# Two float32r pieces instead of three bf16 ones in the last pair's products

## The chip, the cores and the metric

The kernel runs on one core of a Trainium2 chip. The core's engines work side by side, each through its own queue in order: TensorE (PE in the profile; PEld is its weight load), VectorE (DVE), ScalarE (ACT), GpSimd (POOL), and SyncE (SP), which issues most DMAs. The metric is the device time of one execution in microseconds; of several runs the median is given. One further execution was profiled, and all rows of a profile are of that one.

## The reference

Four graph layers run over x, 8 batches of 2048 nodes with 64 features, with one adjacency matrix of 2048 x 2048 for all batches. The first three are attention layers. The last one, which the change is about, is cut to this:

```python
def _L3_gnn_ref(x, w0, b0, wa, ba, adj):
    feat = jax.nn.softplus(x * (INV_SQRT2 * w0[0, 0]) + b0[0])
    scores = feat * wa + ba
    mask = adj > 0
    logits = scores[:, None, :, :] * mask[None, :, :, None].astype(scores.dtype)
    logits = jnp.where(mask[None, :, :, None], logits, jnp.float32(-1000000000.0))
    attn = jax.nn.softmax(logits, axis=2)
    return jnp.einsum('bijd,bjd->bid', attn, feat)

x = _layernorm(x + _L3_gnn_ref(x, ...), axis=-1)
```

The score of a neighbour j depends on j and the feature alone. So softmax and sum become two products of the 0/1 mask: numerator = mask x (feat * exp(score)), denominator = mask x exp(score), for each feature, and the output is their quotient (plus a term for nodes without neighbours), followed by the residual and the layer norm.

## The kernel before, in words

P is 128, N 2048, K = N / P = 16, K2 = 8, F = 64. The mask lies in SBUF as `edge`, fp8, [128, 16, 2048]: block row jb, all target nodes. It is transposed, so that a block `edge[:, jb, ib*128:(ib+1)*128]` can stand in TensorE as the weights for target nodes ib.

The last layer goes by pairs of batches (0,1), (2,3), (4,5), (6,7). `l3_features(b)` (line 1070) computes softplus, exp and their product for one batch into a float32 tile `vf` of [128, 16, 2, 64] (numerator and denominator side by side), and then splits it into three bf16 pieces `v0`, `v1`, `v2`: ScalarE casts to bf16, VectorE or GpSimd subtracts the piece, ScalarE casts the rest, and the second rest is the third piece. GpSimd subtracts for the even batch of a pair, VectorE for the odd one (line 1119). The two batches fill the halves of the same tiles. With a 0/1 mask, three bf16 pieces give nearly the full float32 sum. The pieces of the first three pairs lie in tiles of their own; those of pair (6,7) lie in the `w` buffers (four, of 8 KB per partition), which the attention layers leave free at the end: three of them are taken. The generator waits for that point by `now[0] < 3` (lines 1102 to 1107).

`l3_products` (line 1131) takes a pair when both batches are ready. For each of the 16 blocks ib of target nodes it adds up 16 x 3 products, 128x128 mask block by 256 columns, in one PSUM tile, and ScalarE evicts it to `nd`. After each two blocks `l3_finish` (line 1177) is added to the background work: GpSimd makes `e` (four small operations), VectorE takes the reciprocal, multiplies and adds, ScalarE squares, VectorE reduces, GpSimd takes the power for the inverse deviation, VectorE scales, SyncE sends two DMAs out. During the last pair PSUM tiles come from a pool of two (`alone`).

Order is written out by hand: every stage is a generator, `Streams.step` (line 1219) lets each living one emit its next piece, and `yield n` passes n turns. Each engine's queue holds the instructions in the order of emission, by the helper at line 78, which is why nearly all rows of the profile say L78. A tile with one buffer (such as tag `e`, used by `softplus` and by `l3_finish`) makes the next writer wait for the last reader. The buffers with tag `row` (two, of 8 KB) hold a row broadcast to all partitions in the attention layers (`prepare`, line 725) and are free in the last pair.

Of the kernel before, what the change touches and what calls it, by code (L numbers as in the profile page):

```python
# [7 lines left out]

F32 = mybir.dt.float32
BF16 = mybir.dt.bfloat16  # L10
U8 = mybir.dt.uint8
FP8 = mybir.dt.float8e4
# [2 lines left out]
ALU = mybir.AluOpType  # L15
AX = mybir.AxisListType

P = 128
# [30 lines left out]
def gnn4_kernel(ctx: ExitStack, tc: tile.TileContext, t, out):  # L49
    nc = tc.nc  # L50
    x_in, adjT = t["x"], t["adjT"]
    B, N, F = x_in.shape
    K = N // P
    K2 = K // 2
# [50 lines left out]
    class Banks:  # L105
# [4 lines left out]
        pool = None  # L110
# [26 lines left out]
    vf_slots, nd_slots, o_slots, lo_slots = (Slots(2) for _ in range(4))  # L137

    pe, dve, act, pool = (InOrder(e) for e in (nc.tensor, nc.vector, nc.scalar, nc.gpsimd))

    def psum(name):
        return pm.tile([P, 512], F32, tag="pm", name=name)

# [3 lines left out]
    def bc_k(v, n=K, f=F):  # L147
        return v[:, None, :].to_broadcast([P, n, f])


    ident = consts.tile([P, P], F32, name="ident")
    make_identity(nc, ident)
    ones = consts.tile([P, P], F32, name="ones")
    nc.gpsimd.memset(ones, 1.0)
    mhalf = consts.tile([P, K], F32, name="mhalf")
    nc.gpsimd.memset(mhalf, -0.5)
# [27 lines left out]
    def rows_tile(pool, tag, name, unit=True):  # L184
        return Rows(pool.tile([P, K * F1 + 1], F32, tag=tag, name=name), unit)

# [9 lines left out]
    work = ctx.enter_context(tc.tile_pool(name="work", bufs=2))  # L196
# [3 lines left out]
    def dram_row(name, eng=nc.sync):  # L200
        v = consts.tile([P, F], F32, name=name + "_bc")
        src = t[name]
        eng.dma_start(v, bass.AP(tensor=src.tensor, offset=src.offset, ap=[[0, P], [1, F]]))
        return v
# [9 lines left out]
    src = t["L0_gnn_a"]  # L214
# [6 lines left out]
    p = psum("p_nodes")  # L221
# [26 lines left out]
    edge = consts.tile([P, K, N], FP8, name="edge")  # L248
    te = consts.tile([P, K, NB], BF16, name="te")
    ones3 = consts.tile([3, P], BF16, name="ones3")  # L250
    nc.gpsimd.memset(ones3, 1.0)
    ones_h = consts.tile([P, 2], BF16, name="ones_h")
    nc.gpsimd.memset(ones_h, 1.0)
    zeros_h = consts.tile([P, 2 * K], BF16, name="zeros_h")
    nc.gpsimd.memset(zeros_h, 0.0)
    emptyT = consts.tile([P, 512], BF16, name="emptyT")
    empty = consts.tile([P, K], F32, name="empty")
# [101 lines left out]
    def softplus(f, y, src):  # L359

        act.activation(y, src, AF.Abs, scale=l3c[:, 0:1], bias=l3c[:, 1:2])
        act.activation(y, y, AF.Exp, scale=-1.0)
        yield 1
        act.activation(y, y, AF.Ln, bias=1.0)
        act.activation(f, src, AF.Relu, scale=l3c[:, 0:1], bias=l3c[:, 1:2])
        yield 1
        dve.tensor_tensor(f, f, y, ALU.add)
# [182 lines left out]
    def mean_pieces(sc, total, n):  # L550
# [3 lines left out]
        pm_slots.give()  # L554
        a = sc.mean = small.tile([P, F], BF16, tag="mean3", name=f"mean3_{n}", bufs=B + 1)
        for i in range(2):
# [503 lines left out]
    def l3_mean(q, i, fs, n):  # L1060

        yield from pm_slots.take()
        p = psum(f"p_fm_{n}")
        pe.matmul(p[:, :F], lhsT=ones, rhs=fs, start=True, stop=True)
        yield 1
        q.fm[i] = small.tile([P, F], F32, tag="fm", name=f"fm_{n}", bufs=4)
        dve.tensor_scalar(q.fm[i], p[:, :F], 1.0 / N, -1.0, ALU.mult, ALU.add)
        pm_slots.give()

    def l3_features(b):  # L1070

        if b % 2 == 0:
            q = Pair()
            q.bs, q.n, q.fm, q.ready = [b, b + 1], f"{b}", {}, 0
            pairs.append(q)
        else:
            q = pairs[-1]
        i = b % 2
        n = f"3_{b}"
        yield from vf_slots.take()  # L1080
        yield from e_slots.take()
        yield from h_slots.take()
        f = tmp.tile([P, K, F], F32, tag="h", name=f"f_{n}")
        y = tmp.tile([P, K, F], F32, tag="e", name=f"sp_{n}")
        yield from softplus(f, y, x_cur[b].v)
        e_slots.give()
        v = late.tile([P, K, 2, F], F32, tag="vf", name=f"vf_{n}", bufs=2)
        pool.tensor_tensor(v[:, :, 1], f, bc_k(wa), ALU.mult)
        pool.tensor_tensor(v[:, :, 1], v[:, :, 1], bc_k(l3off), ALU.add)
        fs = small.tile([P, F], F32, tag="fs", name=f"fs_{n}")  # L1090
        dve.tensor_reduce(fs, f.rearrange("p k f -> p f k"), AX.X, ALU.add)
        bg.add(l3_mean(q, i, fs, n))
        yield 2
        act.activation(v[:, :, 1], v[:, :, 1], AF.Exp)
        yield 1
        dve.tensor_tensor(v[:, :, 0], f, v[:, :, 1], ALU.mult)
        h_slots.give()
        yield 1

        if i == 0:  # L1100
            if b == B - 2:
                while now[0] < 3:
                    yield 1
                q.v = [
                    work.tile([P, K, 2, 2, F], BF16, tag="w", name=f"v{m}_{q.n}", bufs=4)
                    for m in range(3)
                ]
            else:
                yield from v_slots.take()
                q.v = [  # L1110
                    late.tile([P, K, 2, 2, F], BF16, tag=f"v{m}", name=f"v{m}_{q.n}")
                    for m in range(3)
                ]
        else:
            while not hasattr(q, "v"):
                yield 1
        act.copy(q.v[0][:, :, i], v)
        yield 1
        eng = dve if i else pool
        eng.tensor_tensor(v, v, q.v[0][:, :, i], ALU.subtract)  # L1120
        yield 1
        act.copy(q.v[1][:, :, i], v)
        yield 1
        eng.tensor_tensor(q.v[2][:, :, i], v, q.v[1][:, :, i], ALU.subtract)
        vf_slots.give()
        yield 1
        q.ready += 1

    K4 = K // 8

    def l3_products():

        while len(pairs) == 0 or pairs[0].ready < 2:
            yield 1
        yield from Banks.share()
        for m in range(B // 2):
            while pairs[m].ready < 2:
                yield 1
            q = pairs[m]
            for ib in range(K):  # L1140
                if ib % K4 == 0:
                    yield from nd_slots.take()
                    q.nd = late.tile(
                        [P, K4, 2, 2, F], F32, tag="nd", name=f"nd_{q.n}_{ib}", bufs=2
                    )
                alone = now[0] == 3
                if alone:
                    p = Banks.pool.tile([P, 1024], F32, tag="b", name=f"p_l3_{q.n}_{ib}")
                else:
                    yield from pl_slots.take()  # L1150
                    p = psum(f"p_l3_{q.n}_{ib}")
                p = p[:, : 4 * F]
                for jb in range(K):
                    for v in q.v:
                        pe.matmul(
                            p,
                            lhsT=edge[:, jb, ib * P : (ib + 1) * P],
                            rhs=v[:, jb].rearrange("p b i f -> p (b i f)"),
                            start=(jb == 0 and v is q.v[0]),
                            stop=(jb == K - 1 and v is q.v[2]),  # L1160
                        )
                    if jb % K2 == K2 - 1:
                        yield 1
                act.activation(
                    q.nd[:, ib % K4],
                    p.rearrange("p (b i f) -> p b i f", b=2, i=2),
                    AF.Identity,
                    bias=empty[:, ib : ib + 1],
                )
                if not alone:  # L1170
                    pl_slots.give()
                if ib % K4 == K4 - 1:
                    bg.add(l3_finish(q, ib // K4, q.nd))
            if m < B // 2 - 1:
                v_slots.give()
# [110 lines left out]
    for n, (layer, b) in enumerate(todo):  # L1286
        if (layer, b) == (2, 1):
            early_.close()
            late = ctx.enter_context(tc.tile_pool(name="late", bufs=1))
            bg.add(l3_products())  # L1290
# [573 lines left out]
```

## Time and profile before

| | us |
|---|---|
| median of 3 runs | 1573.19 (1572.83 to 1574.51) |
| span of the profiled execution | 1572.4 |
| median above that span | 0.8 |
| TensorE busy | 1322.6 (84%) |
| VectorE busy | 1298.6 (83%) |
| ScalarE busy | 801.3 (51%) |
| GpSimd busy | 812.6 (52%) |
| products of the last layer, 3072 records | 353.9 |

Only instructions are profiled, so the profiled execution's own time is its span and the little that lies around it. Times within the profile count from the start of the span. The busy time of TensorE counts overlapping records; the pace of a run of products is read from when they start, or from when ScalarE evicts their result. "Idle before <-releaser" in a row says what an engine waited for.

### The profile page before, as it was taken

The numbers are of one execution on the slowest core, as the hardware profiler recorded it, in microseconds if no ns is written. First come the engines' busy times: TensorE is split into PE (matmuls) and PEld (weight loads), VectorE is DVE, ScalarE is ACT, GpSimd is POOL, SyncE is SP. The second block draws the span as 40 slices with busy tenths as digits, with TensorE's granted clock in tenths as the row PEclk, the third lists the DMA queues.
The fourth block names the chain that finished last, engine by engine and source line by source line (L and its number), as shares of the span: only waits on it lengthen the run. The fifth ranks groups of instructions, "written<-read, shape, count | busy, mean of one in ns | idle before, by whom it ended". The sixth has DMA issues, their size and how long they took to land.

```text
span 1572.4 us, 20954 instructions
## 1 busy us (share of the span) xinstructions
PE 1322.6 (84%) x8130; PEld 657.3 (42%) x8130; DVE 1298.6 (83%) x1364; ACT 801.3 (51%) x1635; POOL 812.6 (52%) x742
## 2 busy tenths in 40 slices
PE   3568989988899899998878575899977989789996
PEld 3213323333333334333222131455543646477885
DVE  4798989988999999999877878978887888777444
ACT  5225445555575434343488667675766575552110
POOL 1144353334234434232576577687879687864332
PEclk8889999999999999999999688899988999889998
DMA  8710000000000000000000000000100000000000
GB/s 325 222 25 1 1 2 1 1 2 2 1 1 2 0 1 2 2 29 27 0 1 27 27 2 27 1 29 7 35 7 34 1 8 8 8 8 15 14 13 18
DMA packets 42190, 36.86 MB, mean 23 GB/s; under 512 B 37509, under 2 KB 37813, under 8 KB 39906
## 3 DMA queue, kind: packets, MB, share of 16 engines
q1 hardware_dynamic: 41538, 34.26, 7.0%
q8 instruction: 66, 1.08, 0.3%
q10 hardware_dynamic: 544, 1.17, 0.2%
q14 instruction: 42, 0.34, 0.1%
HBM read 30.94 MB, written 4.45 MB: 23 GB/s over the span
## 4 chain that ended last, share of the span: by engine, by line
PE 24%; DVE 21%; ACT 9%; issue 4%; POOL 4%; POOLq 0%; DVEq 0%; ACTq 0%
PE p_l L78 16%; DVE w L78 12%; PE acc L78 7%; ACT e L78 4%; DVE o L78 2%; DVE st_x L78 2%; ACT sp L78 1%; POOL w L78 1%; DVE vf L78 1%; ACT x L78 1%; POOL vf L78 1%; ACT v L78 1%; DVE fs L78 1%; POOL e L78 1%; PE p_o L78 1%
## 5 line engine op out<-in xcount | busy, mean ns | idle before, releaser
L78 DVE SCALAR_TENSOR_TENSOR w<-r,se,edge 128x2048 f32<-128x2048 f32 (+1 forms) x270 | 555.6, 2104 | 22.6 <-PE r L78 19.6
L78 PE MATMUL acc<-w,pv 128*64 128x512 f32 x2048 | 502.9, 623 | 74.9 <-DVE w L78 68.2
L78 PEld LDWEIGHTS <-edge 128*128 128x128 fp8e4 x3842 | 322.3, 99 | 124.8 <-issue 66.4
L78 ACT ACTIVATE e<-w,s_g 128x1024 f32<-128x1024 f32 x256 | 277.8, 1113 | 173.2 <-DVE w L78 128.8
L78 PE MATMUL acc<-w,x 128*64 128x512 f32 x1024 | 284.6, 673 | 89.4 <-DVE w L78 84.3
L78 PE MATMUL p_l<-v,edge 128*128 128x256 bf16 x3072 | 353.9, 276 | 0.6 <-ACT nd L78 0.6
L78 DVE TENSOR_TENSOR w<-e,edge 128x1024 f32<-128x1024 f32 x256 | 299.9, 1213 | 50.4 <-ACT e L78 48.7
L78 POOL TENSOR_SCALAR w<-row,hi_g,lo_g 128x2048 f32<-128x2048 f32 x128 | 275.6, 2159 | 42.6 <-PE acc L78 39.6
L78 PEld LDWEIGHTS acc<-w,pv 128*64 128x64 f32 x2048 | 132.0, 140 | 340.7 <-issue 182.5
L78 PEld LDWEIGHTS acc<-w,x 128*64 128x64 f32 x1024 | 64.4, 146 | 239.2 <-DVE w L78 170.7
L78 ACT ACTIVATE nd<-p_l,empty 128x256 f32<-128x256 f32 x64 | 29.9, 469 | 132.9 <-PE p_l L78 132.9
L78 ACT ACTIVATE x<-o,st_x 128x64 f32<-128x64 f32 x256 | 90.3, 444 | 4.2 <-DVE st_x L78 4.2
L78 ACT COPY oT<-acc 128x512 f32<-128x512 f32 x48 | 25.7, 587 | 126.8 <-PE acc L78 126.8
L78 ACT ACTIVATE o<-p_o,den 128x64 f32<-128x64 f32 x256 | 56.0, 326 | 49.9 <-DVE den L78 49.7
L78 POOL TENSOR_TENSOR st_h<-isw_h,mhalf 128x16 f32<-128x16 f32 x8 | 23.9, 2982 | 106.6 <-DVE isw_h L78 81.7
L78 PE MATMUL p_o<-rh,oT 128*128 128x130 f32 x384 | 60.5, 295 | 20.4 <-DVE st L78 13.2
L78 POOL TENSOR_TENSOR st_x<-isw_x,mhalf 128x16 f32<-128x16 f32 x24 | 71.1, 2964 | 2.0
L78 PEld LDWEIGHTS p_o<-rh,oT 128*128 128x128 f32 x384 | 49.8, 197 | 52.1 <-issue 32.9
L78 DVE TENSOR_REDUCE st<-sq 128x4 f32<-128x256 f32 x32 | 13.2, 414 | 65.2 <-ACT sq L78 65.1
L78 POOL TENSOR_SCALAR isw_x<-isw_x 128x16 f32<-128x16 f32 x24 | 6.3, 263 | 113.5 <-DVE isw_x L78 113.5
L78 POOL CAST rT<-rT 16x128 bf16<-16x128 f32 x45 | 15.1, 335 | 94.6 <-ACT rT L78 91.5
L78 POOL TENSOR_SCALAR isw<-isw 128x4 f32<-128x4 f32 x32 | 7.4, 231 | 104.1 <-DVE isw L78 99.5
(236 smaller groups left out, 1516.5 us busy)
## 6 DMA issues: line engine op xcount, KB each, us to landing
raw<-in_adjT_dram SPq DMA_DIRECT2D x8, 1024.0 KB
raw<-in_adjT_dram SPq DMA_DIRECT2D x16, 512.0 KB
row<-rows_d_g SPq DMA_DIRECT2D x8, 1024.0 KB
x<-in_x_dram SPq DMA_DIRECT2D x8, 512.0 KB
out_dram<-o SPq DMA_DIRECT2D x64, 64.0 KB
row<-row_d ACTq DMA_DIRECT2D x1, 1024.0 KB
row_d<-rT SPq DMA_DIRECT2D x15, 12.0 KB
row<-row_d SPq DMA_DIRECT2D x15, 12.0 KB
```

Source lines behind the costliest of these rows:

```text
L78: ins = f(*args, **kwargs)
```

## The change

For the last pair alone, `l3_features` now makes two pieces, each split in two tiles of half the blocks (four tiles of 8 KB, so all four `w` buffers), of type float32r, a 4-byte type with fewer mantissa bits: ScalarE casts both halves once, VectorE subtracts both halves, for both batches. The products need both operands in that type, so the mask block of each ib (128 x 2048 elements) is cast from fp8 to float32r by a new function `widen`, even ib on ScalarE, odd ib on GpSimd, into the two `row` buffers, one block ahead of its use. The products of this pair are 16 x 2 per ib instead of 16 x 3. In the program a float32r product is a single instruction that brings its weights itself, where the bf16 product has a weight load of its own ahead of it. The other pairs are unchanged; their loop moves into `products`.

```diff
+F32R = mybir.dt.float32r
...
                 q.v = [
-                    work.tile([P, K, 2, 2, F], BF16, tag="w", name=f"v{m}_{q.n}", bufs=4)
-                    for m in range(3)
+                    [
+                        work.tile([P, K2, 2, 2, F], F32R, tag="w", name=f"v{m}_{h}_{q.n}", bufs=4)
+                        for h in range(2)
+                    ]
+                    for m in range(2)
                 ]
...
+        if b >= B - 2:
+            for h in range(2):
+                act.copy(q.v[0][h][:, :, i], v[:, h * K2 : (h + 1) * K2])
+            yield 1
+            for h in range(2):
+                dve.tensor_tensor(
+                    q.v[1][h][:, :, i],
+                    v[:, h * K2 : (h + 1) * K2],
+                    q.v[0][h][:, :, i].bitcast(F32),
+                    ALU.subtract,
+                )
+            vf_slots.give()
+            yield 1
+            q.ready += 1
+            return
...
+    wide = {}
+
+    def widen(ib):
+
+        if ib < K:
+            m = work.tile([P, K, P], F32R, tag="row", name=f"mask_{ib}")
+            src = edge[:, :, ib * P : (ib + 1) * P]
+            if ib % 2:
+                pool.tensor_copy(m, src)
+            else:
+                act.copy(m, src)
+            wide[ib] = m
+
+    def products(p, q, ib, jb):
+
+        if q.bs[1] == B - 1:
+            for m in range(2):
+                pe.matmul(
+                    p,
+                    lhsT=wide[ib][:, jb],
+                    rhs=q.v[m][jb // K2][:, jb % K2].rearrange("p b i f -> p (b i f)"),
+                    start=(jb == 0 and m == 0),
+                    stop=(jb == K - 1 and m == 1),
+                )
+            return
+        for v in q.v:
+            pe.matmul(
+                p,
+                lhsT=edge[:, jb, ib * P : (ib + 1) * P],
+                rhs=v[:, jb].rearrange("p b i f -> p (b i f)"),
+                start=(jb == 0 and v is q.v[0]),
+                stop=(jb == K - 1 and v is q.v[2]),
+            )
...
             q = pairs[m]
+            if m == B // 2 - 1:
+                widen(0)
             for ib in range(K):
+                if m == B // 2 - 1:
+                    widen(ib + 1)
...
                 for jb in range(K):
-                    for v in q.v:
-                        pe.matmul(
-                            p,
-                            lhsT=edge[:, jb, ib * P : (ib + 1) * P],
-                            rhs=v[:, jb].rearrange("p b i f -> p (b i f)"),
-                            start=(jb == 0 and v is q.v[0]),
-                            stop=(jb == K - 1 and v is q.v[2]),
-                        )
+                    products(p, q, ib, jb)
                     if jb % K2 == K2 - 1:
                         yield 1
```

## The prediction

> **What bounds the kernel now.** I read the chain of waits in order of time first, because only its last stretch can belong to the pair of batches that the change touches. The long pieces of its end:
>
> ```profile
> 1403.58 4.03 POOL vf L78
> 1407.63 1.90 ACT v L78
> 1417.22 1.92 DVE fs L78
> 1419.87 138.93 PE p_l L78 x1248
> ```
>
> From 1419.87 us TensorE alone carries the end: 1248 products in a row, with nothing between them. Before that the chain goes through GpSimd (a subtraction of the value pieces of batch 6), ScalarE and VectorE, and the change touches that too. Next, busy time by stretch (PE, PEld, DVE, ACT, POOL with counts, clock, DMA):
>
> ```profile
> 1425.21:1474.80 49.59, 49.59 (x456) 44.46 (x455) 29.26 (x55) 9.50 (x16) 17.00 (x30) 1.00 0.07 15
> 1474.80:1558.60 83.80, 83.80 (x770) 75.03 (x767) 38.10 (x80) 10.03 (x24) 26.28 (x48) 1.00 0.06 14
> 1558.60:1572.40 13.80, 0.18 (x2) 0.00 (x0) 6.33 (x16) 1.20 (x3) 4.55 (x8) 0.61 0.11 24
> ```
>
> The second row is the last pair: TensorE is full at full clock, and ScalarE (12%) and GpSimd (31%) have room. The third is the drain after the last product. ScalarE's evictions in the timeline give the pace:
>
> ```profile
> 1474.98 0.47 ACT L78 ACTIVATE nd<-p_l,empty 128x256 f32<-128x256 f32 x1 [4.77 <-PE p_l L78]
> 1480.22 0.47 ACT L78 ACTIVATE nd<-p_l,empty 128x256 f32<-128x256 f32 x1 [4.46 <-PE p_l L78]
> ```
>
> One row block each 5.24 us; divided by its 48 products that is 109.2 ns, whatever the 273 ns of one record say (they overlap). The pair costs 16 x 5.24 = 83.84 us.
>
> No float32r product is in this trace. Its nearest kin are float32 products, in TensorE's timeline and its weight loads' (a run of instructions each, with its length):
>
> ```profile
> 563.24 0.97 PEld L78 LDWEIGHTS p_s<-as,xTv 128*128 128x128 f32 x8 [0.81 <-issue]
> 563.24 1.06 PE L78 MATMUL p_s<-as,xTv 128*128 128x4 f32 x8
> 608.63 1.94 PE L78 MATMUL acc<-w,pv 128*64 128x512 f32 x8 [0.67 <-ACT oT L78]
> ```
>
> The p_s products stream only 4 columns, so their weight loads set the pace: (0.97 - 0.19) / 7 = 0.111 us per load of 128 float32 columns, 0.19 being one load. The products p_o with 130 columns run at the same 0.11 us (8 in 1.16 us), so a load does hide behind the stream before it. The acc run is 4 products of 512 columns, each in two records, two at a time side by side: (1.94 - 0.59) / 3 = 0.45 us per record, 0.88 ns a column. The bf16 stream takes 109 / 256 = 0.43 ns a column; call that one cycle, and float32 takes two, twice.
>
> **What the Trainium skill says.** FP8 and Floating Point Precision, TensorE Precision Notes: full float32 takes four passes, the reduced form reads 4-byte values and truncates them. The acc run (two records, each two cycles a column) agrees on the four; that the reduced form is one pass of one cycle a column is my reading, shown by no row. TensorE: Matmul & The Clock Gate, Weight-path perf modes: the fast weight load is off for float32. The trace agrees: a 128-column load lasts 190 ns in p_s and 98 ns for the fp8 mask. Same page, What's actually happening: after an idle window of some 3.4 us the clock halves. Here idle stretches of 2.2 to 2.5 us were already mostly followed by 3.4 us at half clock, and the one of 3.83 us at 1415.35 by 6.83 us.
>
> **The change part by part.**
>
> *1. Products.* 48 become 32 per row block, 768 become 512. Each streams 256 columns, the same 109 ns if one cycle a column, with a weight load of 111.7 ns (bound from above by p_s) behind it: I take 111.7. 512 x 0.1117 = 57.2 us instead of 83.84: **-26.65**. From both sides: 109 ns if the loads are faster (another -1.4); 216 ns if 4-byte values stream at two cycles a column, as p_xT's transposes do (8 of 128 columns in 1.09 us).
>
> *2. Mask casts, eight by ScalarE, eight by GpSimd, two buffers.* ScalarE: its cast of 128x2048 (v<-vf) lasts 1.90 us; the page ScalarE: Activation LUTs (What ACT_TABLE_LOAD costs) gives 186 + 0.833 x 2048 ns = 1.89 for the same. Cast ib+1 waits for the last product of ib-1, which is when block ib starts. ScalarE first evicts (0.47): done some 2.6 us into a block of 3.57. Hidden, with 0.9 us to spare; behind a cast that still waits stands only the next eviction, which needs a later product anyway. GpSimd shows no such cast; its one-input pass of the same size:
>
> ```profile
> L78 POOL TENSOR_SCALAR w<-row,hi_g,lo_g x128: 2040/2047/3245, 767.9 to 1351.2; 128x2048 f32<-128x2048 f32 x128
> ```
>
> I take 2.1 us. The floor: GPSIMD Engine Reference, section 3.1, has bodies with few operations at 1.03 cycles an element, at its 1.2 GHz an estimated 1.8 us. The ceiling is the two-input pass here, 4.07 us. GpSimd's queue for two blocks (7.15 us) then holds 2.1 + 0.23 + 1.04 (the power) + 4 x 0.52 (e) = 5.5 us. Behind a waiting cast stand isw and the power of the former rows, and behind those VectorE's scaling and the output; they have 1.4 us to spare. The cover is gone at a cast of about 3.2 us; at 4.07 two blocks take 4.07 + 0.3 + 3.57 = 7.95, +0.8 us seven times. Taken: **0** (ceiling +5.6).
>
> *3. The hand-over to the last pair.* Cast 0 is queued on ScalarE behind the eviction of the former pair's last block (its order in the program, not a need of data). So TensorE stops at 1474.78, the eviction starts at 1474.98, the cast about 0.37 later and ends at 1477.25, the first product starts near 1477.4: **+2.6**. Cast 1 has no such wait. A gap of 2.6 us should bring one 3.4 us window at half clock: **+1.7** (0 to 3.4).
>
> *4. Value pieces.* For batch 6 GpSimd loses two subtractions (4.06 and 4.07 us); VectorE gets two halves (1024 elements, 1.21 each). ScalarE casts two halves once instead of a whole tile twice, and its second cast no longer waits at 1407.63 for GpSimd:
>
> ```profile
> 1407.75 1.58 PE L78 MATMUL p_l<-v,edge 128*128 128x256 bf16 x13
> 1409.95 5.40 PE L78 MATMUL p_l<-v,edge 128*128 128x256 bf16 x48 [0.62 <-ACT nd L78]
> 1419.18 0.69 PE L78 MATMUL p_fm<-fs,ones 128*128 128x64 f32 x2 [3.83 <-DVE fs L78]
> ```
>
> In TensorE's timeline the stop of 0.62 is the eviction behind that cast, the stop of 3.83 the mean of batch 7, which waits for the softplus queued on ScalarE. Its first step (1409.80) then waits only for buffer e, freed by VectorE: 1402.78 + 2 x 1.2 (the new halves) + 1.74 + 0.43 + 0.43 = 1407.8 (the 3.40 us of o<-nd at 1404.48 was contention with GpSimd's subtraction). All that follows moves 2.0 us ahead: the mean at 1417.2, **-2.0** (0 to -4). TensorE then stands 2.8 us instead of 0.62 + 3.83, so one half-clock window instead of two: **-1.6** (0 to -3.3). Batch 7's single round of pieces, and the fourth w buffer, end long before 1474.78, where they are needed (v<-vf at 1433.3 was the last): 0; without that cover some 2 us.
>
> *5. Drain.* Same instructions after the last eviction, 13.6 us: 0. No DMA is added.
>
> Sum: -26.65 + 0 + 2.6 + 1.7 - 2.0 - 1.6 = -25.95 against the profiled 1572.4: 1546.4 us. The median of the runs is 0.8 above the span: **1547.2**, given as 1547.
>
> **The rivals.**
>
> *A. The stream takes two cycles a column.* For it: p_xT, the only one-record float32 stream here, does. Against it: a transpose has to deliver the whole float32 value, and acc's four passes leave a quarter for one. 512 x 0.216 = 110.6 us, +26.8 instead of -26.65: 1600.7 us. Its place is the last pair's stretch, and it decides from 162 ns per product on ((83.84 - 2.6 - 1.7 + 2.0 + 1.6) / 512). Chance 0.15.
>
> *B. GpSimd's cast becomes the bound.* For it: every second block waits on it, in a queue with the power and four adds. Against: 2.05 us for the pass of the same size. Ceiling +5.6: 1553 us; with a cast slower still than two-input work, up to 1560. Chance 0.10.
>
> *C. Weight loads don't hide* (the instruction loads its own weights, so there is no separate load to pull ahead). Against: p_o hides them. 109 + 55 to 109 + 111 ns: 84 to 113 us, 1574 to 1603. Chance 0.04.
>
> *D. The change doesn't do what it says*: float32r runs as full float32, 4 x 109 ns: 223 us, about 1713. The program lists one product, not two, for each. Chance 0.02.
>
> **How the numbers follow.** My forecast has 0.69; its own range is 1541 (cheap loads, no half-clock windows) to 1553. With B the range 1541 to 1566 holds about 0.8. Within 0.2% (about 3 us, what a measurement tells from no change) lies only the low end of C: 0.02. Faster 0.79 (forecast and B), slower 0.19 (A, D, most of C).
>
> **What would show it.** Row blocks in the evictions 3.6 us apart (right), 6.9 (A) or alternating 3.6 and 4.4 (B, with TensorE idle until GpSimd's mask). LDWEIGHTS of the mask near 190 ns at a pitch of 112. One stop of TensorE of 2.6 us before the first product of the last pair, ended by ScalarE's mask. p_fm of batch 7 near 1417. The forecast is wrong if the pitch isn't within 109 to 120 ns or if TensorE stops anywhere inside the last pair.

## The result and the profile after

The changed kernel takes 1552.48 us (median of 4 runs, 1550.31 to 1554.46) against 1573.01 for the kernel before in the same runs; the ratio is 0.9865, with a 95% interval of 0.9828 to 0.9902. It is faster, by 20.5 us, where 26 had been forecast.

The chain of waits of the changed kernel in order of time, its end (start, length, what):

```profile
1401.17 2.81 DVE v L79 x2
1414.10 1.91 DVE fs L79
1416.49 54.08 PE p_l L79 x480
1470.97 1.90 ACT mask L79
1472.91 61.71 PE p_l L79 x512
```

GpSimd's subtraction has left the chain, VectorE's two halves have come in, and the run of products is now cut once, by ScalarE's cast of mask block 0. Busy time by stretch of the changed kernel (PE, PEld, DVE, ACT, POOL with counts, clock, DMA), the same three stretches as before:

```profile
1419.90:1470.40 50.50, 50.50 (x464) 45.14 (x462) 30.82 (x58) 8.04 (x17) 19.91 (x34) 1.00 0.08 17
1472.90:1534.60 61.70, 61.69 (x512) 61.49 (x512) 42.69 (x80) 22.06 (x30) 39.69 (x55) 1.00 0.08 18
1534.60:1548.50 13.90, 0.00 (x1) 0.00 (x0) 6.33 (x16) 1.20 (x3) 4.55 (x8) 0.67 0.10 24
```

The pair now takes 61.7 us instead of 83.8, and its weight loads (second figure) fill the stretch too. The rest of the core is far from full: ScalarE 22 of 61.7 us, GpSimd 39.7. The timeline of ScalarE's evictions gives the pace:

```profile
1477.05 0.48 ACT L79 ACTIVATE nd<-p_l,empty 128x256 f32<-128x256 f32 x1 [3.87 <-PE p_l L79]
1480.88 0.48 ACT L79 ACTIVATE nd<-p_l,empty 128x256 f32<-128x256 f32 x1 [1.58 <-PE p_l L79]
1484.72 0.47 ACT L79 ACTIVATE nd<-p_l,empty 128x256 f32<-128x256 f32 x1 [3.06 <-PE p_l L79]
```

A row block takes 3.84 us; divided by 32 that is 120 ns a product, not the 111.7 of the forecast. The instructions on the mask tiles:

```profile
L79 PEld LDWEIGHTS p_l<-v,mask x512: 186/192/192, 1472.9 to 1534.2; 128*128 128x128 f32 x171
L79 PE MATMUL p_l<-v,mask x512: 279/283/384, 1472.9 to 1534.3; 128*128 128x256 f32 x171
L79 POOL CAST mask<-edge x8: 1885/1892/1892, 1465.2 to 1527.0; 128x2048 fp32r<-128x2048 fp8e4 x8
L79 ACT CAST mask<-edge x8: 1887/1892/1897, 1471.0 to 1523.5; 128x2048 fp32r<-128x2048 fp8e4 x8
```

One record per product, and 120 ns from one to the next: here float32r is a single pass. Both engines cast a block in 1.89 us. TensorE's timeline at the two places where it stops:

```profile
1416.06 0.43 PE L79 MATMUL p_fm<-fs,ones 128*128 128x64 f32 x2 [3.19 <-DVE fs L79]
...
1472.91 57.26 PE L79 MATMUL p_l<-v,mask 128*128 128x256 f32 x475 [2.35 <-ACT mask L79]
```

By stages of the two profiled executions (marks: the last product of the attention layers' sums `acc` ends; p_fm, the mean of batch 7's features, starts; the pair's first product starts; its last one starts; the end):

| stage | before | after | difference |
|---|---|---|---|
| to the last attention product | 1364.46 | 1362.94 | -1.5 |
| to p_fm of batch 7 | 54.72 | 53.12 | -1.6 |
| to the pair's first product | 55.60 | 56.85 | +1.25 |
| the pair | 83.73 | 61.41 | -22.3 |
| drain | 13.89 | 14.18 | +0.3 |
| span | 1572.4 | 1548.5 | -23.9 |

The first row lies ahead of everything that the change moves. In later executions of variants that are equal up to there it ended anywhere from 1361.4 to 1367.0, so it is spread between executions. The third row is the stop at the hand-over (+2.35) against a shorter stretch at half clock around p_fm (3.4 us instead of 6.8), which gives back some 1.1 us.

### The profile page after: what moved, and what is told of

It is laid out like the page before. It is cut to its first block, busy times and chain, and to the rows that moved or that the text cites. A ratio compares the mean times of both kernels' runs of the same rounds, so it can differ in the third digit from the quotient of the medians.

```text
span 1548.5 us, 20475 instructions
## 1 busy us (share of the span) xinstructions
PE 1303.4 (84%) x7874; PEld 645.7 (42%) x7874; DVE 1300.8 (84%) x1366; ACT 812.4 (52%) x1643; POOL 820.2 (53%) x748
## 4 chain that ended last, share of the span: by engine, by line
PE 23%; DVE 22%; ACT 9%; issue 4%; POOL 3%; POOLq 0%; DVEq 0%; ACTq 0%
PE p_l L79 15%; DVE w L79 12%; PE acc L79 7%; ACT e L79 4%; DVE o L79 2%; DVE st_x L79 2%; ACT sp L79 1%; DVE vf L79 1%; ACT x L79 1%; PE p_o L79 1%; POOL w L79 1%; DVE nd L79 1%; ACT v L79 1%; DVE fs L79 1%; POOL vf L79 1%
## 5 line engine op out<-in xcount | busy, mean ns | idle before, releaser
L79 PEld LDWEIGHTS <-edge 128*128 128x128 fp8e4 x3074 | 246.1, 99 | 116.1 <-issue 65.9
L79 PE MATMUL p_l<-v,edge 128*128 128x256 bf16 x2304 | 267.9, 276 | 0.0
L79 PE MATMUL p_l<-v,mask 128*128 128x256 f32 x512 | 61.7, 283 | 2.4 <-ACT mask L79 2.4
L79 PEld LDWEIGHTS p_l<-v,mask 128*128 128x128 f32 x512 | 61.5, 192 | 2.6 <-ACT mask L79 2.6
```

The costliest lines, as they stand in the source:

```text
L79: ins = f(*args, **kwargs)
```

## The experiments

The theory: the gain is the 256 products that are gone; the pieces give a little, the hand-over takes a little, and float32r itself only costs. Its rivals: the gain comes from ScalarE no longer waiting for GpSimd, or from float32r. Beside it stood the question of the 120 ns.

### The changed kernel again

> The changed kernel itself once more, as the level for its neighbours here. Both theories: 1550 to 1554 us, ratio to before 0.985 to 0.988. In the profile the 512 float32r products at a pitch of 120 ns, TensorE standing about 2.4 us before the first of them.

1553.4 us, ratio 0.9869 (0.9847 to 0.9891), pitch (from the start of one product to the next) 120 ns, stop 2.35 us. In its profile p_fm comes 53.12 us after the last attention product and the pair takes 61.41 us, both as in the first. The level holds; the experiments are compared with this and with the first result.

### Two bf16 pieces, no float32r

```diff
-                    for m in range(3)
+                    for m in range(2)
...
+        if b >= B - 2:
+            dve.tensor_tensor(q.v[1][:, :, i], v, q.v[0][:, :, i], ALU.subtract)
+            vf_slots.give()
+            yield 1
+            q.ready += 1
+            return
...
-                            stop=(jb == K - 1 and v is q.v[2]),
+                            stop=(jb == K - 1 and v is q.v[-1]),
```

> The last pair in two bf16 pieces, made as in the change (ScalarE casts once, VectorE subtracts), no third piece: less precise, no float32r, no mask casts. Theory P (the gain is the 256 products that are gone, float32r only costs): 512 products at 109 ns, 55.9 us for the pair instead of 61.4, no stop before it, so some 7 to 8 us below the changed kernel, near 1544. Theory Q (float32r itself or the casts bring the gain): not below the changed kernel.

1542.98 us, ratio 0.982 (0.9797 to 0.9843). Busy time of this run in the stretch of the pair:

```profile
1470.40:1526.40 56.00, 56.00 (x514) 50.04 (x512) 38.07 (x80) 10.01 (x24) 26.26 (x48) 1.00 0.09 20
```

512 products in 56 us (109 ns each), and TensorE does not stop before them. It is 10 us below the changed kernel by the medians; by the stages of the profile 5.6 in the pair and 2.5 ahead of it. So the gain is the number of products (theory P): float32r with its casts costs some 8 us of what two pieces save. What it is meant to buy is precision, since a bf16 piece has fewer bits; no run here measured how much.

### The pieces alone

```diff
-        eng = dve if i else pool
+        eng = dve if i or b >= B - 2 else pool
```

> The kernel before with one part of the change: in the last pair VectorE makes both subtractions of batch 6 too, GpSimd none; still three bf16 pieces. Theory P: the small part of the gain, the mean of batch 7 some 1.5 us earlier and at most one half-clock window less: 1 to 4 us below before. Theory R (most of the gain comes from ScalarE no longer waiting for GpSimd): 10 us or more below before.

1570.9 us, ratio 0.9985 (0.9974 to 0.9995). TensorE's timeline of this run:

```profile
1408.80 5.73 PE L78 MATMUL p_l<-v,edge 128*128 128x256 bf16 x51
1417.38 0.43 PE L78 MATMUL p_fm<-fs,ones 128*128 128x64 f32 x2 [2.85 <-DVE fs L78]
```

The short stop of 0.62 us is gone, the other is 2.85 us instead of 3.83, and p_fm comes 52.8 us after the last attention product instead of 54.7. Theory P's 1 to 4 us; theory R's 10 us are excluded by the interval (0.8 to 4.1 us).

### Cast 0 one block earlier

```diff
-            if m == B // 2 - 1:
-                widen(0)
             for ib in range(K):
+                if m == B // 2 - 2 and ib == K - 1:
+                    widen(0)
```

> The changed kernel with mask cast 0 queued on ScalarE one row block earlier, ahead of the eviction of the former pair's last block. Theory H (the stop of 2.4 us at the hand-over is that queue order alone): the stop is gone, the pair starts 2.4 us earlier, 1.5 to 4 us below the changed kernel. Rival: TensorE then waits for something else there (the eviction of an older block, cast 1), and the time stays within 1 us of the changed kernel.

1546.95 us, ratio 0.9836 (0.9812 to 0.9859). ScalarE's and TensorE's timelines of this run:

```profile
1466.16 0.47 ACT L79 ACTIVATE nd<-p_l,empty 128x256 f32<-128x256 f32 x1 [4.46 <-PE p_l L79]
1466.53 1.89 ACT L79 CAST mask<-edge 128x2048 fp32r<-128x2048 fp8e4 x1
1471.40 0.47 ACT L79 ACTIVATE nd<-p_l,empty 128x256 f32<-128x256 f32 x1 [2.98 <-PE p_l L79]
```

```profile
1466.83 4.53 PE L79 MATMUL p_l<-v,edge 128*128 128x256 bf16 x40
1471.12 9.12 PE L79 MATMUL p_l<-v,mask 128*128 128x256 f32 x74
```

The cast now runs while TensorE works on the former pair's last block, and the first float32r product follows without a stop. From p_fm to the pair's start it is 54.26 us instead of 56.85: 2.6 us, theory H. The medians differ by more (6.5 us, the intervals overlap); that excess is not explained by any stage of the profile.

### Products of 128 columns, with and without the stop

```diff
-                pe.matmul(
-                    p,
-                    lhsT=wide[ib][:, jb],
-                    rhs=q.v[m][jb // K2][:, jb % K2].rearrange("p b i f -> p (b i f)"),
...
+                for b in range(2):
+                    pe.matmul(
+                        p[:, b * P : (b + 1) * P],
+                        lhsT=wide[ib][:, jb],
+                        rhs=q.v[m][jb // K2][:, jb % K2, b].rearrange("p i f -> p (i f)"),
...
```

> The changed kernel with each float32r product of 256 columns cut into two of 128 (one per batch), 64 instead of 32 per row block, same results. It shows the floor that the self-brought weight load sets. Theory L (the load is mostly hidden; 120 ns is a stream of 107 with some 13 ns of overhead): the pitch falls only to the load's floor, 110 to 120 ns, the pair takes 64 x 16 x 0.112 = 115 us instead of 61.4, about +53 us on the changed kernel. Rival M (the load isn't the floor, the stream alone is): pitch near 60 to 75 ns, 61 to 77 us, 0 to +15 us.

1705.7 us, ratio 1.0835: +152 us on the changed kernel, three times what theory L gave. Busy time of this run in two stretches of the pair, where the last three columns are clock, DMA share and GB/s:

```profile
1474.70:1520.00 45.30, 45.30 (x215) 45.30 (x214) 9.32 (x17) 5.30 (x6) 8.36 (x13) 0.50 0.03 7
1520.00:1680.00 160.00, 160.00 (x752) 160.00 (x751) 32.42 (x60) 16.45 (x23) 31.05 (x42) 0.50 0.02 6
```

The clock is at a half from 1.1 us after the pair's first product to its last, although TensorE is never idle; a product takes 213 ns. All four runs lie between 1700.9 and 1706.7 us. The next run has the same products and the early cast of the run before.

> The 128-column products again, now without the stop at the hand-over, to tell what halved the clock through the whole pair in the former run. Theory T (the stop's one half-clock window, from which products that stream half of the time never recover): clock at full from the start, pitch 107 to 112 ns, 110 to 115 us for the pair. Theory U (128-column float32r products lower the clock by themselves): the clock halves within some 5 us of the pair's start and stays, pitch 213, 216 us for the pair.

1603.88 us (one run). The same view:

```profile
1480.00:1520.00 40.00, 40.00 (x361) 40.00 (x360) 13.18 (x25) 9.13 (x12) 12.93 (x17) 1.00 0.04 9
1520.00:1580.00 60.00, 60.00 (x539) 60.00 (x539) 24.09 (x46) 12.17 (x16) 23.34 (x33) 1.00 0.05 10
```

Full clock from the first product to the last, 539 products in 60 us, 111 to 112 ns each, 114.3 us for the pair. So the stop of 2.35 us costs 102 us here (theory T, on one run of the second kernel): it halves the clock, and these products, in which the stream of 128 columns is only half of the 213 ns (256 columns take 213 ns at half clock, see the 512-column run below), never bring it back. At full clock the 115 us of the first run's theory L come out, and 112 ns is the floor that the weight load sets: half the stream saves only 8 of 120 ns.

### Products of 512 columns

```diff
...
-            for m in range(2):
-                pe.matmul(
...
+            pe.matmul(
+                p,
+                lhsT=wide[ib][:, jb],
+                rhs=q.v[jb // 4][:, jb % 4].rearrange("p m b i f -> p (m b i f)"),
...
+                if m == B // 2 - 1:
+                    dve.tensor_tensor(
+                        q.nd[:, ib % K4],
+                        q.nd[:, ib % K4],
+                        p[:, 4 * F :].rearrange("p (b i f) -> p b i f", b=2, i=2),
+                        ALU.add,
+                    )
```

> The changed kernel with both pieces side by side as one moving operand of 512 columns, 16 products per row block instead of 32, sums in two halves of a PSUM bank, which VectorE adds after the eviction (16 more VectorE adds). Theory F (13 ns per instruction over the stream): pitch 213 + 13 = 227 ns, 58.0 us for the pair, -3.4 us. Theory S (4-byte values stream slower, 0.47 ns a column): pitch 240, no change of the products. Theory L0 (it was the load, now fully hidden): pitch 216, 55.3 us, -6. VectorE's adds, some 0.45 us each, cost nothing in all of these unless its queue (6.3 of 7.7 us for two blocks) becomes the bound.

1548.8 us, ratio 0.984 (0.9812 to 0.9867). TensorE's timeline of this run:

```profile
1477.06 53.14 PE L79 MATMUL p_l<-v,mask 128*128 128x512 f32 x226 [2.35 <-ACT mask L79]
```

226 to 227 ns from one start to the next at full clock (the row above holds a stretch of 3.4 us at half clock too, so the whole pair takes 59.6 us). What the stream alone takes can be worked out from the half-clock stretches: there the bf16 products of 256 columns start 213 ns apart (1418.4 to 1425.2 us of the kernel before), so 256 columns take 107 ns at full clock, 2 ns less than those products' 109 there, and 512 take 213. That is theory F, about 13 ns over the stream at 256 and at 512 columns. Theory S, a slower stream, is out.

### The second piece in bf16

```diff
+            pe.matmul(
+                p,
+                lhsT=wide[ib][:, jb],
+                rhs=q.v[0][jb // K2][:, jb % K2].rearrange("p b i f -> p (b i f)"),
...
+            pe.matmul(
+                p,
+                lhsT=edge[:, jb, ib * P : (ib + 1) * P],
+                rhs=q.v[1][:, jb].rearrange("p b i f -> p (b i f)"),
...
```

> The changed kernel with the second piece in bf16 against the fp8 mask, the first in float32r against the cast mask: in turn one of each, 32 per row block. Theory F or S (the float32r product itself costs 120): mean pitch (120 + 109) / 2 = 114.5 ns, 58.6 us for the pair, -2.8 us. Theory L (the float32r load behind a float32r stream is what costs): the float32r load now runs behind a bf16 stream and the fp8 load behind the float32r stream; if the load is the cost whatever it hides behind, again 114.5, if it is only its clash with a float32r stream, 109, 55.9 us, -5.5.

1552.88 us, ratio 0.9872 (0.985 to 0.9894). Both theories fell. TensorE's timeline of this run:

```profile
1489.80 0.28 PE L79 MATMUL p_l<-v,edge 128*128 128x256 bf16 x1
1489.84 0.36 PE L79 MATMUL p_l<-v,mask 128*128 128x256 f32 x1
1490.04 0.28 PE L79 MATMUL p_l<-v,edge 128*128 128x256 bf16 x1
1490.08 0.36 PE L79 MATMUL p_l<-v,mask 128*128 128x256 f32 x1
```

One of each takes 0.24 us (243 to 244 ns over longer stretches), where two float32r products take 240 and two bf16 products 218. The pair is 62.4 us, not 58.6. Alternating the types gives back the 11 ns that the bf16 product saves and 3 to 4 more; why was not tried.

### Half of the weight columns

```diff
+                r = P // 2 if 0 < jb < K - 1 else P
                 pe.matmul(
-                    p,
-                    lhsT=wide[ib][:, jb],
+                    p[:r],
+                    lhsT=wide[ib][:, jb, :r],
...
-                    bias=empty[:, ib : ib + 1],
+                    bias=ones[:, 0:1] if m == B // 2 - 1 else empty[:, ib : ib + 1],
```

> The changed kernel with cast 0 early, and in the last pair all products but those of the first and last mask block of a row take half of the weight columns (64 of 128): half of the last pair's sums are left out, and a constant 1 stands in for the term of empty nodes. Theory L (the 13 ns above 107 depend on the float32r load): with half a load the pitch falls to about 109 ns. Theory F (a fixed cost of each float32r product): it stays at 120.

1547.01 us (one run of a kernel that leaves out half of the last pair's sums). The instructions on the product tile in this run:

```profile
L79 PEld LDWEIGHTS p_l<-v,mask x512: 133/134/192, 1472.1 to 1530.5; 128*64 128x64 f32 x149, 128*128 128x128 f32 x22
L79 PE MATMUL p_l<-v,mask x512: 274/276/362, 1472.1 to 1530.6; 128*64 128x256 f32 x149, 128*128 128x256 f32 x22
```

The products with 64 weight columns start 113 to 114 ns apart, those with 128 at 118 to 120. With 107 ns for the stream, the rest is 13 ns with 128 weight columns and 6.5 with 64, about 0.1 ns per weight column. Neither expectation was met in full; a fixed cost (theory F) is out, and the load (theory L) is the likely reading. It is not shown alone: half of the weight columns also means half of the rows of the result, and the mix above shows a cost that no load explains.

### All casts but the first by GpSimd

```diff
-            if ib % 2:
+            if ib:
                 pool.tensor_copy(m, src)
```

> The changed kernel with all mask casts from block 1 on by GpSimd, none but the first by ScalarE: tests the room left in GpSimd's queue. By the forecast's sum two blocks hold 2 x 1.89 + 0.23 + 1.04 + 2.15 = 7.2 us of 7.68: still hidden, within 2 us of the changed kernel. Rival B (GpSimd's casts are near to being the bound): its queue delays masks, TensorE waits for GpSimd at every other block, +5 us or more.

1554.87 us, ratio 0.9891 (0.9867 to 0.9915), within 2 us or so of the changed kernel. Busy time of this run inside the pair:

```profile
1480.00:1530.00 50.00, 49.98 (x411) 49.41 (x411) 43.39 (x62) 8.30 (x20) 43.98 (x49) 1.00 0.08 17
```

GpSimd works 44 of 50 us. What ended the idle time ahead of the instructions on the mask tiles:

```profile
  PE p_l L79: 4.0, 5
  POOL mask L79: 0.6, 3
```

TensorE's weight loads wait for GpSimd's mask three times, 0.6 us in all, where they never do so in the changed kernel. So the cover that hides the casts is just used up with twice the casts that the change gives GpSimd; rival B's 5 us are out. The pair takes 63.8 us instead of 61.4; most of the difference is a stretch of 3.4 us at half clock.

### What helped, together

512 columns and the early cast in one kernel.

> The two changes that each helped, together: 512-column float32r products and mask cast 0 queued one block earlier. If they add up: products at 227 ns, no stop at the hand-over, the pair in 58.0 us; 1572.4 - 83.84 + 58.0 with 3 us from the pieces gives 1543 to 1546, some 8 us below the changed kernel. If ScalarE or VectorE becomes the bound at 3.6 us a block instead (rival): blocks further apart than 3.65 us, no lower than 1548.

1545.78 us, ratio 0.9827 (0.981 to 0.9843). The instructions on the product tile in this run:

```profile
L79 PE MATMUL p_l<-v,mask x256: 387/389/476, 1468.7 to 1526.7; 128*128 128x512 f32 x128
L79 ACT ACTIVATE nd<-p_l,empty x64: 451/473/477, 1008.8 to 1527.1; 128x256 f32<-128x256 f32 x64
L79 DVE TENSOR_TENSOR nd<-nd,p_l x16: 406/417/425, 1473.2 to 1528.0; 128x256 f32<-128x256 f32 x16
```

The pair takes 58 us as forecast, starts without a stop, and the adds of 0.42 us hide, but for the last, which can only come after the last product. It beats both kernels, with the same two float32r pieces as the changed one; against the early cast alone the medians (1.2 us apart) don't settle it, the pair's 58 against 61.4 us does. The lowest median remains that of two bf16 pieces (1542.98 us, the intervals overlap; 55.9 us for the pair), with fewer bits in its pieces.

## Why the prediction was right, and where its terms were off

The direction, the cause and the range held; 1547.2 was 5.3 us too low. Of these, 2.1 lie between the forecast's span and the profiled one, and 3.2 in what was added for the median of the runs. It was right with little to spare: 1552.5 us lies at the upper end of its own 1541 to 1553, and the pitch of 120 ns at the end of the 109 to 120 ns that it set as its limit.

1. *Products.* The count was right, one pass and one cycle a column was right, the size was off: -22.3 us in place of -26.65. The forecast took the larger of load (111.7) and stream (109). p_o, its ground for "a load does hide", has both at about 111 ns (the load by p_s, the stream as 130 columns at twice 0.43 ns), so it couldn't show a part left over. The runs with 512 columns and with 64 weight columns showed one: 13 ns on top of the stream of 107, so 120 in place of 111.7, and 512 x 8.3 ns = 4.2 us.
2. *Mask casts.* 0, right; 1.89 us on GpSimd instead of the 2.1 taken. The run with twice its casts, where the cover just ran out, shows that it was there.
3. *Hand-over.* The stop was 2.35 us for 2.6, shown by the early cast to be queue order. The half-clock window behind it (+1.7, 0 in its range) did not come in this execution, nor in the second profile of the changed kernel nor in the mix; with the same stop it came in the profiles of the 128-column run, the 512-column run and the GpSimd casts. The clock records of the traces show what decides. The granted clock changes only at the ends of pieces of 3.41 us (between the first and the last change, each stretch at one clock is a whole number of them), and where these pieces lie differs from execution to execution. In the three profiles where the clock fell, one piece held 2.27 to 2.31 us of the stop; in the three where it stayed, the stop lay across the end of a piece, and the longer part was 1.36, 1.72 and 1.79 us. So which of the two an execution gets is chance, and by these six the term was worth about half of the 1.7.
4. *Pieces.* p_fm 1.6 us earlier for 2.0. The path was right: softplus's first step starts when VectorE has freed buffer e (at 1406.67 us in the changed kernel), but VectorE's two halves took 2.81 us instead of 2 x 1.2, and that is the 0.4 us. The half-clock stretch was 3.4 us for 6.8, as forecast, worth some 1.1 us instead of 1.6. The part alone measured 2.6 us (0.8 to 4.1). In the second profile of the changed kernel the half-clock stretch was 6.8 us again.
5. *Drain.* From the start of the last product 14.2 us for 13.9, right.

The sum on the profiled executions is -23.9, of which -1.5 is not the change's; the change's own -22.4 stand against -25.95. The median of the runs lay 4 us above the span of the profiled one, where before it lay 0.8 above, and the forecast took that difference over unchanged. Every run with both on record has a time of 1.75 to 1.93 us above its span. So the profile before, at 1572.4, was of an execution of some 1574.2 us, among the slower of runs from 1570.65 to 1574.51, and that of the changed kernel was the fastest of its four: the two profiles lie further apart than the medians.

Of the rivals, A (two cycles a column) fell by the 120 ns and the 227 ns at 512 columns. Its ground was weak: p_xT's pace of 109 ns for 128 columns is so near the load's (111 ns in p_s) that it can't tell a slow stream from a load; the float32r products of 128 columns run at 112 ns too. B fell by the changed kernel's profile, in which no product waits for GpSimd, D by the single record and its 120 ns. C (loads don't hide) was right in about an eighth, if the 13 ns are the load's: 13 of 112.

## What to carry to other kernels

Price a change of type on TensorE as products times pitch, with the load and the stream taken from rows where they differ; where they happen to be equal, a row can't show whether one hides the other in full. When the work on the critical engine is handed to new operands, look at what the first of them is queued behind: here one cast behind an eviction cost 2.4 us and was free one block earlier. Don't price a stop of TensorE by its length alone, since the clock may follow it down. And before paying for a wider type, ask what the pieces are for: two bf16 pieces were 10 us faster than two float32r ones.

## What the runs showed of the hardware that was not expected

- A stop of 2.35 us ahead of products that stream for only half of their time (128 columns against a 112 ns load) left the clock at a half for 216 us of uninterrupted work, 1705.7 us in all; without the stop the same products ran at full clock throughout, 1603.9 us (one run).
- The same stop of 2.35 us halved the clock in three of six profiles: in those in which one 3.41 us piece of the clock's record held at least 2.27 us of it, and not in those in which no piece held more than 1.79.
- A float32r product takes 13 ns over its stream with 128 weight columns, at 256 and at 512 moving columns alike, and 6.5 ns with 64 (at 256); alternating float32r and bf16 products takes 243 to 244 ns for two, more than two float32r ones (240), and why stays open.
- GpSimd's cast of 128x2048 from fp8 to float32r takes the same 1.89 us as ScalarE's.
